# Masks of the second scores as rank-32 step products, and a plan with ranks for single operations

## The chip, the cores and the metric

The kernel runs on one core of one Trainium2 chip. The time is device microseconds from the start of the program to its end, smaller is better. Three timed runs of the kernel before are shown, and one more execution that was profiled.

## The reference

One transformer layer on x of shape (1, 4096, 256), float32: local attention with a post-norm, then a gated feed-forward part with a post-norm.

```python
# attention: 16 query heads in 4 groups, head size 16; each group has one key and one value head
q, k, v = x @ Wq + bq, x @ Wk + bk, x @ Wv + bv          # k, v: 4 heads of 16
scores = q @ k.T / sqrt(16)
mask   = (i - 128 >= j) | (i < j)                        # each query sees itself and the 127 before it
att    = softmax(where(mask, -1e9, scores)) @ v
x      = layernorm(x + att @ Wo + bo)
# feed-forward: each row is mixed with the row before it
xr, xk = mu_r * x + (1 - mu_r) * x_prev, mu_k * x + (1 - mu_k) * x_prev
out    = sigmoid(xr @ W_r.T) * (square(relu(xk @ W_k.T)) @ W_v.T)
x      = layernorm(x + out)
```

## The kernel before

The 4096 rows are cut into 32 blocks of 128 and these into 16 pairs; four blocks (512 rows) are a chunk. Per chunk the kernel transposes x (`xT`, L560), makes keys and values (`kv`, L583) and queries (`q`, L631), transposes the values (`vT`, L606), and moves every second query head 16 partitions up with four DMAs (`q move`, L653).

Scores are computed twice. The **first time** ("maxima", L686 to L708) they lie with queries on partitions, so that VectorE can take each row's maximum over the keys (`reduce`, L718). The negated maxima are transposed and stored by four DMAs into a row of qT (`nm put`, L732), where they act as one more element of the contraction, next to a row of ones in kT. The **second time** ("weights", L775 and L787) keys lie on partitions. The product with 17 rows then gives score minus maximum, transposed, and ScalarE only has to apply exp (L827, L855). For a block of 128 queries there are three kinds of second scores: its own keys and the previous block's keys as far as they are full width (`weights a`, one block of 128 queries, 512 columns), and the rest for two blocks together (`weights b`, L837 on, two halves of 256 columns). The exps go into the product with the values (`values`, L882 and L895), whose extra column of ones gives the denominators.

The mask of the second scores is added on TensorE. Before the product, small bf16 matmuls write 0 or -2^30 into the same PSUM columns: `identZ` (a 32 x 32 identity with 32 columns of zeros on one side) as weights spreads a mask tile (`maskOwn`, `maskPrev`, `maskNone`) into the even or odd 32 keys of the 64. There are two such passes, E and O, for each half of 64 keys and each of four head groups. A pass that masks the whole of one query tile besides the step of another has 256 columns, one that has the step alone 128.

All of this works on TensorE in tiles: row tiles of 32 by column tiles of 64 in the second scores (eight matmuls side by side), 32 by 128 in the maxima, 128 by 32 in the values, and full width in the rest.

The order of work is written by a planner (`Plan`, L141 on) when the program is built. Each operation is entered with `op`, with an engine, a length and a rank from the table `KINDS`, and with what it reads, writes and needs of buffers (`Ring`) and PSUM banks (`Banks`, eight). `run` plays a schedule through: on each engine, of the operations that could start within `WAIT` or `PE_WAIT` of the earliest, it takes the one of lowest rank; a change of tiling on TensorE costs `TURN`, 0.2. The instructions of every engine stand in this order and execute in it; the planner's times are nowhere in the program. SyncE (SP) issues nearly all DMAs in this order too. `rest` is one operation there: the three weights of the feed-forward part, Wo in four pieces, and bo.

In L775 and L787 the lines that matter are these:

```python
masks = ((intoE, maskOwn[:, 1:2], lo, 1), (intoO, maskOwn[:, 0:2], lo, 2))      # own keys
masks = ((intoE, maskPrev[:, 0:2], lo, 2), (intoO, maskPrev[:, 0:1], lo + RQ, 1))  # previous keys
```

The third entry is the first column, the fourth the number of 128-column tiles that a mask matmul writes.

Of the kernel before, what the change touches and what calls it, by code (L numbers as in the profile page):

```python
# [11 lines left out]
ALU = mybir.AluOpType  # L12
# [22 lines left out]
    "w": (PE, 0.43, -14.24),  # L35
    "w copy": (ACT, 0.62, 3.74),
    "x load": (SP, 0.5, -8.79),
    "x first": (SP, 3.3, -12.27),
    "x second": (SP, 2.5, -8.28),
    "xT": (PE, 0.43, 0.69),  # L40
    "xT copy": (ACT, 0.6, 5.02),
    "kv": (PE, 1.72, -6.04),
    "kv copy": (ACT, 0.69, -12.31),
    "vT": (PE, 0.43, -3.72),
    "vT copy": (DVE, 0.4, 1.8),
    "ones": (SP, 0.1, -12.06),
    "q": (PE, 1.72, -2.77),
    "q copy": (ACT, 0.69, -9.26),
    "q move": (SP, 2.0, -9.27),
    "maxima": (PE, 0.93, -1.84),  # L50
    "maxima 2": (PE, 0.66, -2.01),
    "reduce": (DVE, 1.14, 1.56),
    "reduce 2": (DVE, 0.81, -16.65),
    "nm turn": (DVE, 0.21, -6.03),
    "nm put": (SP, 2.0, 5.46),
    "weights a": (PE, 1.1, -0.52),
    "exp a": (ACT, 1.02, -9.82),
    "weights b": (PE, 1.3, -0.14),
    "exp b": (ACT, 1.02, 8.26),
    "values": (PE, 2.7, 0.67),  # L60
    "oN": (DVE, 1.25, -2.26),
    "rs": (DVE, 0.35, 9.56),
    "at": (DVE, 0.9, -0.26),
    "attT": (DVE, 0.44, 3.73),
    "xres": (SP, 0.5, -7.25),
    "bo": (POOL, 1.3, 19.18),
    "wo": (PE, 1.72, 2.61),
    "y": (DVE, 0.69, 9.88),
    "x1T first": (POOL, 0.25, 21.46),
    "x1T": (PE, 0.43, 3.16),  # L70
    "x1T copy": (ACT, 0.6, 10.29),
    "xd": (POOL, 1.3, -1.75),
    "xm": (DVE, 0.45, 27.04),
    "fk": (PE, 1.72, 6.41),
    "relu": (ACT, 0.6, 4.81),
    "square": (POOL, 1.07, 27.6),
    "fr": (PE, 1.72, 7.15),
    "gate": (ACT, 0.6, 13.52),
    "fv last": (PE, 0.86, 37.29),
    "y2 last": (DVE, 0.42, 26.45),  # L80
    "stats last": (DVE, 1.0, 21.07),
    "scale last": (POOL, 1.05, -29.88),
    "apply last": (DVE, 0.46, -15.48),
    "fv": (PE, 1.72, 3.74),
    "y2": (DVE, 0.69, -0.64),
    "y2 add": (POOL, 1.3, -4.68),
    "store": (SP, 0.5, -2.34),
    "rest": (SP, 4.5, 9.89),
    "stats y": (DVE, 0.6, 9.58),
    "scale y": (POOL, 1.5, 16.27),  # L90
    "apply y": (ACT, 0.6, 3.08),
    "stats y2": (DVE, 0.6, 10.75),
    "scale y2": (POOL, 1.5, -23.39),
    "apply y2": (ACT, 0.6, 23.42),
# [46 lines left out]
class Plan:  # L141
# [7 lines left out]
    WAIT = 0.39  # L149
    PE_WAIT = 0.20  # L150
    TURN = 0.2

    def __init__(self):
        self.ops = []
        self.writer, self.readers = {}, {}
        self.users, self.taker = {}, {}
        self.banks = Banks()

    def op(self, kind, base, fn, r=(), w=(), uses=(), new=(), banks=(), mode=None):
# [5 lines left out]
        rank += base  # L165
# [19 lines left out]
        self.ops.append((eng, length, rank, fn, deps, list(new), list(banks), mode))  # L185

    def run(self):
# [40 lines left out]
        while cand:  # L228
            best = {}
            for i in cand:  # L230
# [11 lines left out]
                turn = self.TURN if e == PE and ops[i][7] != last_mode else 0.0  # L242
# [9 lines left out]
            eng, length, _, fn, _, new, banks, mode = ops[i]  # L252
# [8 lines left out]
            land = eng == SP  # L261
            free[e] = s + length
            end[i] = s + (self.LAND + length if land else length)
            order.append((s, len(order), i))
            for k in nexts[i]:
                hop = 0.0 if ops[k][0] == eng and not land else self.DRAIN if eng == PE else self.HOP
                if ops[k][0] == PE and eng == PE:
                    hop = 0.0
                ready[k] = max(ready[k], end[i] + hop)
                left[k] -= 1  # L270
                if not left[k]:
                    cand.add(k)
# [7 lines left out]
def postln_block(  # L280
# [197 lines left out]
    identZ = const.tile([P, 3, Q], BF16, tag="identZ", name="identZ")  # L478
    nc.vector.memset(identZ, 0.0)
    nc.vector.tensor_copy(identZ[:, 1, :], identR[:, 0, :])  # L480
    intoE = identZ[:, 1:3, :].rearrange("p a b -> p (a b)")
    intoO = identZ[:, 0:2, :].rearrange("p a b -> p (a b)")


    nc.vector.tensor_tensor(diag, diag, after, ALU.add)
    four = diag.to_broadcast([P, GS, Q])
    maskOwn = const.tile([P, 2, GS, Q], BF16, tag="maskOwn", name="maskOwn")
    maskPrev = const.tile([P, 2, GS, Q], BF16, tag="maskPrev", name="maskPrev")
    nc.vector.memset(maskOwn[:, 0, :, :], NEG)
    nc.vector.memset(maskPrev[:, 1, :, :], NEG)  # L490
    nc.vector.tensor_scalar(maskOwn[:, 1, :, :], four, -NEG, NEG, ALU.mult, ALU.add)
    nc.vector.tensor_scalar(maskPrev[:, 0, :, :], four, NEG, None, ALU.mult)
    maskNone = const.tile([P, T], BF16, tag="maskNone", name="maskNone")
    nc.vector.memset(maskNone, NEG)
# [17 lines left out]
    def load_rest():  # L512
        for k, w in (("r", W_r), ("k", W_k), ("v", W_v)):
            load_w(ffn_l[k], w)
        for g in range(NG):
            nc.sync.dma_start(
                out=wo[32 * g : 32 * (g + 1), :, :],
# [810 lines left out]
```

## Time and profile before

| | |
|---|---|
| median of 3 timed runs | 356.84 us (355.78 to 358.21) |
| profiled execution, its own time | 357.12 us |
| span of the profile, first to last instruction | 355.4 us |
| TensorE busy (5091 matmuls) | 342.9 us, 96% |
| VectorE, ScalarE, GpSimd busy | 244.8, 179.0, 125.8 us |
| granted TensorE clock, mean | 0.99 |

PE is TensorE, PEld its weight loads (they overlap the matmuls), DVE VectorE, ACT ScalarE, POOL GpSimd, SPq the DMA issues of SyncE. A row of groups reads: line, engine, operation, tiles written and read, shapes, count, then busy time and mean ns of one, then idle time just before them and what ended it. A row of the timeline reads: start and length in us, engine, line, operation and count; rows of several instructions that run side by side are merged. A row of the windows reads: from and to, length, busy time (and number of instructions) of PE, PEld, DVE, ACT and POOL, granted TensorE clock, DMA share, GB/s. An fp32 matmul stands as two instructions. [...]

### The profile page before, as it was taken

The page shows a single profiled execution, that of the slowest core. Times are in us where ns is not written, and L with a number is a line of the kernel's source. Part 1 is how long each engine was busy: PE and PEld are TensorE (multiplying, and loading weights), DVE is VectorE, ACT ScalarE, POOL GpSimd, SP SyncE. Part 2 cuts the span into 40 slices and gives each one's busy share as a digit, 9 for nine tenths or more (in the row PEclk, how much of TensorE's full clock was granted, in tenths as well). Part 3 has the DMA queues.
Part 4 walks back from the last instruction along what each step waited for, and adds up shares of the span by engine and source line. Part 5 has one row for each costly group of instructions (what it writes and reads, how often), then busy time and mean ns, then how long its engine had stood idle before and what let it go on. Part 6 is the DMA issues. An engine that isn't in the chain of part 4 may idle for free.

```text
span 355.4 us, 11751 instructions
## 1 busy us (share of the span) xinstructions
PE 342.9 (96%) x5091; PEld 230.2 (65%) x5091; DVE 244.8 (69%) x464; ACT 179.0 (50%) x253; POOL 125.8 (35%) x223
## 2 busy tenths in 40 slices
PE   6999999999999999999999999999999999999982
PEld 5655565566747676767657676766757676667871
DVE  4146474888593898988927987388845888548554
ACT  3423537273537284647355554737456373863441
POOL 5110000412234363534315251253505352626883
PEclk9989999999999999999999999999999999999997
DMA  6855150140004101102223020320205020200011
GB/s 187 260 88 77 50 92 5 32 64 5 8 29 34 61 33 33 50 16 58 66 21 73 5 61 5 31 61 4 63 3 83 16 60 5 61 4 0 31 59 60
DMA packets 34518, 17.34 MB, mean 49 GB/s; under 512 B 20734, under 2 KB 34434, under 8 KB 34466
## 3 DMA queue, kind: packets, MB, share of 16 engines
q1 hardware_dynamic: 34288, 16.46, 20.5%
q8 instruction: 40, 0.66, 0.8%
q10 hardware_dynamic: 178, 0.13, 0.1%
q14 instruction: 12, 0.10, 0.1%
HBM read 9.97 MB, written 4.19 MB: 40 GB/s over the span
## 4 chain that ended last, share of the span: by engine, by line
PE 91%; DMA 3%; DVE 2%; ACT 1%; SPq 1%; POOL 1%; issue 1%; POOLq 0%; DVEq 0%; ACTq 0%
PE ps L1144 15%; PE ps L787 13%; PE ps L708 10%; PE ps L882 9%; PE ps L1021 8%; PE ps L631 8%; PE ps L1118 7%; PE ps L895 5%; PE ps L775 4%; PE ps L583 4%; PE ps L1054 3%; PE ps L695 2%; PE ps L560 2%; PE ps L606 1%; DMA qT<-qT 1%; DMA x<-in_L_attn_x 1%
## 5 line engine op out<-in xcount | busy, mean ns | idle before, releaser
L718 DVE TENSOR_REDUCE nm<-ps 128x6 f32<-128x960 f32 (+1 forms) x96 | 94.0, 1034 | 21.3 <-PE ps L708 20.9
L827 ACT ACTIVATE prA<-ps 128x1024 f32<-128x1024 f32 x64 | 61.7, 1023 | 38.1 <-PE ps L787 35.2
L787 PE MATMUL ps<-qT,kT 17*64 17x256 f32 (+1 forms) x1024 | 57.6, 495 | 0.0
L708 PE MATMUL ps<-kT,qT 16*128 16x160 f32 x1024 | 46.0, 305 | 0.4 <-DMA qT<-qT 0.4
L1176 POOL TENSOR_TENSOR y<-y,x 128x512 f32<-128x512 f32 x15 | 20.9, 1394 | 59.3 <-DVE y L1171 59.3
L708 PEld LDWEIGHTS ps<-kT,qT 16*128 16x128 f32 x1024 | 37.4, 185 | 2.7 <-issue 1.3
L966 POOL TENSOR_SCALAR ve_y<-mv_y 128x2 f32<-128x2 f32 x31 | 8.0, 257 | 87.6 <-DVE mv_y L961 87.3
L1090 DVE SCALAR_TENSOR_TENSOR xm<-xd,vecs,x1T 128x256 f32<-128x256 f32 x64 | 34.3, 582 | 1.4 <-POOL xd L1082 1.4
L855 ACT ACTIVATE prB<-ps 128x1024 f32<-128x1024 f32 x32 | 31.2, 1034 | 3.8 <-PE ps L787 3.8
L631 PE MATMUL ps<-xT,wq 128*128 128x512 f32 x64 | 32.4, 631 | 0.0
L1021 PE MATMUL ps<-wo,attT 128*128 128x256 f32 x128 | 31.6, 389 | 0.0
L882 PE MATMUL ps<-prA,vA 128*32 128x256 f32 x512 | 30.9, 382 | 0.6 <-DVE nm L718 0.6
L960 DVE BATCH_NORM_STATS2 st_y<-y 128x6 f32<-128x256 f32 x62 | 25.3, 408 | 8.7 <-POOL y L1176 8.2
L1082 POOL TENSOR_TENSOR xd<-x1T 128x512 f32<-128x512 f32 x16 | 16.6, 1041 | 40.6 <-ACT x1T L1067 40.6
L775 PEld LDWEIGHTS <-identZ 32*64 32x64 bf16 x1024 | 18.2, 104 | 19.5 <-issue 18.5
L1118 PE MATMUL ps<-xm,wkT 128*128 128x256 f32 x128 | 30.3, 380 | 0.3 <-ACT prB L855 0.3
L1144 PE MATMUL ps<-wrT,xm 128*128 128x256 f32 x128 | 30.4, 380 | 0.0
L1144 PE MATMUL ps<-wvT,kact 128*128 128x256 f32 x120 | 29.4, 387 | 0.8 <-ACT sig L1158 0.8
L1144 PEld LDWEIGHTS ps<-wvT,kact 128*128 128x128 f32 x120 | 22.0, 190 | 11.6 <-issue 7.5
L1012 POOL TENSOR_TENSOR xres<-xres,bo_b 128x512 f32<-128x512 f32 x16 | 20.4, 1278 | 25.2 <-DMA xres<-in_L_attn_x 13.7
L1021 PEld LDWEIGHTS ps<-wo,attT 128*128 128x128 f32 x128 | 23.2, 190 | 7.9 <-ACT prA L827 5.3
L1031 DVE TENSOR_TENSOR y<-ps,xres 128x512 f32<-128x512 f32 x16 | 11.1, 691 | 23.0 <-PE ps L1021 17.5
(99 smaller groups left out, 511.3 us busy)
## 6 DMA issues: line engine op xcount, KB each, us to landing
x<-in_L_attn_x SPq DMA_DIRECT2D x16, 256.0 KB
xres<-in_L_attn_x SPq DMA_DIRECT2D x16, 256.0 KB
out<-res SPq DMA_DIRECT2D x15, 256.0 KB
qT<-qT SPq DMA_DIRECT2D x32, 64.0 KB
qT<-nmT SPq DMA_DIRECT2D x64, 4.0 KB
wl_xk<-in_L_attn_Wq SPq DMA_DIRECT2D x1, 256.0 KB
wl_xr<-in_L_ffn_W_r SPq DMA_DIRECT2D x1, 256.0 KB
wl_xr<-in_L_ffn_W_k SPq DMA_DIRECT2D x1, 256.0 KB
```

Source lines behind the costliest of these rows:

```text
L631: nc.tensor.matmul(ps, wq[:, ch, rp, :, :].rearrange("p g x -> p (g x)"), xT[c][:, ch, :], start=(ch == 0), stop=(ch == C2 - 1),)
L708: nc.tensor.matmul(sc[g // 2][:, g % 2, u * W : (u + 1) * W], qT[c][g0 : g0 + DH, (2 * p + j) % NB, s, :, :].rearrange("p r i -> p (r i)") ...
L718: nc.vector.tensor_reduce(nms[p % 2].rearrange("p g j s -> p g (j s)")[:, 2 * i : 2 * i + 2, lo:hi], two_banks(keys[i])[:, :, 0 : n * W].r ...
L775: nc.tensor.matmul(dst[g][:, lo : lo + n * RQ], into[q, :], maskNone[q, 0 : n * RQ] if m is None else m[q].rearrange("p s r i -> p (s r i) ...
L787: nc.tensor.matmul(dst[g], kT[k, k0 : k0 + 64], qT[c][k, blk, r0 : r0 + nr, :, :].rearrange("p s r i -> p (s r i)"), start=False, stop=Tru ...
L827: nc.scalar.activation(prA[b][:, 2 * i : 2 * i + 2, :], two_banks(keys[i]), AF.Exp)
L855: nc.scalar.activation(prB[p][:, 2 * i : 2 * i + 2, :, :].rearrange("p g j n -> p g (j n)"), two_banks(keys[i]), AF.Exp,)
L882: nc.tensor.matmul(av[32 * g : 32 * (g + 1), hf, j, :], vA[:, values_of(b, g)], prA[b][:, g, hf * H : (hf + 1) * H], start=(j == 0), stop= ...
L1021: nc.tensor.matmul(ps[:, j, :], attT[2 * p + j][:, rp, :, :].rearrange("p s i -> p (s i)"), wo[:, rp, :], start=(rp == 0), stop=(rp == 1),)
L1090: nc.vector.scalar_tensor_tensor(dst[p][:, ch, :], st["d"][:, ch, :], muT[:, which, ch : ch + 1], x1T[p][:, ch, 0:H2], ALU.mult, ALU.add,)
L1118: nc.tensor.matmul(ps[:, o, :], ffnT["k"][:, ch, o * P : (o + 1) * P], xk[p][:, ch, :], start=(ch == 0), stop=(ch == C2 - 1),)
L1144: nc.tensor.matmul(ps[:, b, :], lhs[:, ch, b * P : (b + 1) * P], w[:, ch, :], start=(ch == 0), stop=(ch == C2 - 1),)
```

## The change

The masks of the second scores are written in another way. Where before each 32 keys of a 64-key half got their own mask tile, now the weights of the mask matmul are a step matrix over 64 keys (`step`, or its complement `back`), and the moving tile is one and the same: -2^30 times the identity, repeated (`negR`). A product of the two masks, for one query tile, all 64 keys at once. A half of 64 keys still takes two such products (for the first and for the second query tile of the pair that touches it), each of 128 columns in `weights a`. In `weights b` both blocks of the pair are masked by the same matmul, of 2 x 128 columns, and its two halves become one block of masks followed by one block of products. The first query block, which has no previous keys, gets a whole mask (`put_all`).

In the planner the lengths of the two weights kinds are 0.92 and 1.1 instead of 1.1 and 1.3, a weights block directly after another one costs `DRY` (0.3), `WAIT` and `PE_WAIT` are wider, DMA lengths differ, all ranks are new, and TensorE's operations get a rank for each single one from a table `ADJUST`. The one `rest` load is cut into five operations (W_k, W_r, W_v, Wo, bo), each of which the planner places by itself, and each reader waits for its own.

In the program that comes out, TensorE has 776 mask matmuls in its second scores (528 of 128 columns, 244 of 256, 4 of 512) instead of 1024 (504 of 128, 512 of 256, 8 of 512), the rest of its work is the same in number and shape, and its order is another: the two `weights a` and the `weights b` of a pair, which mostly stood close together (15 times a `weights a` directly ahead of another weights block), now have other work between them (4 times). There are 153 changes of tiling instead of 128. At the start SP issues both xres loads, x tiles 2 to 5, Wo, the ones, the move of q, x tiles 6 to 9, W_k, W_r, W_v, bo, and then the first `nm put`; before, the three weights, Wo and bo stood ahead of the move of q. The transposes of the three weights come after the first maxima instead of ahead of them.

```diff
 KINDS = {
-    "weights a": (PE, 1.1, -0.52),
-    "weights b": (PE, 1.3, -0.14),
-    "rest": (SP, 4.5, 9.89),
+    "weights a": (PE, 0.92, -3.74),
+    "weights b": (PE, 1.1, -0.16),
+    "rest": (SP, 1.4, 29.33),
+    "rest wo": (SP, 2.0, 28.31),
+    "rest bo": (SP, 0.8, 34.95),
...
+ADJUST = {
+    "weights b": [
+        -8.25, -1.85, -1.15, -1.05, -0.05, 0.8, 1.25, -5.4, -5.55, -4.35, 4, 0.4, 1.95, 2.15, 9.15, -12.25,
+    ],
...
-        rank += base
+        n = self.count[kind] = self.count.get(kind, -1) + 1
+        rank += base + (ADJUST[kind][n] if kind in ADJUST else 0)
...
+    def turn(self, before, after):
+        return self.TURN if before != after else self.DRY if after == "32x64" else 0.0
...
-    identZ = const.tile([P, 3, Q], BF16, tag="identZ", name="identZ")
...
-    maskNone = const.tile([P, T], BF16, tag="maskNone", name="maskNone")
-    nc.vector.memset(maskNone, NEG)
+    step = const.tile([P, 4, Q], BF16, tag="step", name="step")
+    back = const.tile([P, 4, Q], BF16, tag="back", name="back")
+    nc.vector.memset(step[:, 0, :], 0.0)
+    nc.vector.tensor_copy(step[:, 1, :], after[:, 0, :])
+    nc.vector.memset(step[:, 2:4, :], 1.0)
+    nc.vector.tensor_scalar(back, step, -1.0, 1.0, ALU.mult, ALU.add)
+    negR = const.tile([P, NS, GS, Q], BF16, tag="negR", name="negR")
+    nc.vector.tensor_scalar(
+        negR.rearrange("p s r i -> p (s r) i"), diag.to_broadcast([P, NS * GS, Q]), NEG, None, ALU.mult
+    )
+    FIRST, SECOND, ALL = slice(Q, 3 * Q), slice(0, 2 * Q), slice(2 * Q, 4 * Q)
...
+    def put_masks(dst, own, first, second, start=(True, True)):
+        for i, (part, cols) in enumerate(((FIRST, first), (SECOND, second))):
+            for h in range(len(dst)):
+                for g in range(len(dst[h])):
+                    q = slice(32 * g, 32 * (g + 1))
+                    d = dst[h][g][:, :, cols[h] : cols[h] + RQ]
+                    nc.tensor.matmul(
+                        d,
+                        flat(step if own[h] else back)[q, part],
+                        negR[q, 0 : d.shape[1], :, :].rearrange("p s r i -> p s (r i)"),
+                        start=(i == 0 and start[h]),
+                        stop=False,
+                        skip_group_check=True,
+                    )
...
-            half_scores(b, [two_banks(k) for k in keys], slice(0, T), ((1, 0, NS), (0, 0, NS)), True)
+            sc = [two_banks(k) for k in keys]
+            dst = [[sc[g // 2][64 * h : 64 * (h + 1), g % 2, :] for g in range(NG)] for h in range(2)]
+            if b:
+                put_masks(
+                    [[d.rearrange("p (o n) -> p o n", o=1) for d in half] for half in dst],
+                    (True, False), (0, 2 * RQ), (RQ, 3 * RQ),
+                )
...
+            for h in range(2):
+                put_scores(dst[h], b, h, 1 - h, 0, NS)
...
+            if p:
+                put_masks(dst, (False, True), (0, 0), (RQ, RQ))
...
             for j in range(2):
-                half_scores(
-                    2 * p + j,
...
+                for h in range(2):
+                    put_scores([d[:, j, :] for d in dst[h]], 2 * p + j, h, h, 2 * h, 2)
...
-        op("w", base, turn, r=["rest"], w=[("wps", k)], banks=[(key, 1)], mode="full")
+        op("w", base, turn, r=[("rest", k)], w=[("wps", k)], banks=[(key, 1)], mode="full")
...
-            op("rest", 0, load_rest, w=["rest"])
+            for k in ("k", "r", "v", "bo", "wo"):
+                op("rest" if k in ffn_l else "rest " + k, 0, lambda k=k: load_rest(k), w=[("rest", k)])
```

`put_scores` is the old product loop (L787) as a function of its own, `put_all` one mask matmul per head group over all columns.

## The prediction

> **What bounds the kernel now.** I read the page first (engines, slices, chain), then the groups of instructions by shape, then the timeline of one steady stretch on TensorE, then the windows and queues of the start.
>
> ```profile
> span 355.4 us, 11751 instructions
> PE   6999999999999999999999999999999999999982
> PE 91%; DMA 3%; DVE 2%; ACT 1%; SPq 1%; POOL 1%; issue 1%; POOLq 0%; DVEq 0%; ACTq 0%
> ```
>
> The chain that ended last is 91% TensorE, and from the second slice to the last but one TensorE never rests. The windows say it more sharply: from 100 to 300 us it is busy 199.98 of 200. So every nanosecond of its stream is path, and work on the other engines counts only where TensorE must wait for it. The groups of the second scores (masks L775, products L787):
>
> ```profile
> L787 PE MATMUL ps<-qT,kT 17*64 17x512 f32 x512 | 34.9, 599 | 0.0
> L787 PE MATMUL ps<-qT,kT 17*64 17x256 f32 x512 | 22.9, 391 | 0.0
> L775 PE MATMUL ps<-maskPrev,identZ 32*64 32x256 bf16 x248 | 19.2, 280 | 0.0
> L775 PE MATMUL ps<-maskOwn,identZ 32*64 32x256 bf16 x256 | 18.6, 267 | 0.0
> L775 PE MATMUL ps<-maskOwn,identZ 32*64 32x128 bf16 x256 | 16.4, 227 | 0.0
> L775 PE MATMUL ps<-maskPrev,identZ 32*64 32x128 bf16 x248 | 15.0, 213 | 0.0
> ```
>
> 70 us of mask matmuls is not 70 us of path: eight run side by side (four row groups, two column groups). What they cost is seen only in the order of starts:
>
> ```profile
> 120.84 0.25 PE L775 MATMUL ps<-maskOwn,identZ 32*64 32x128 bf16 x4
> 120.85 0.30 PE L775 MATMUL ps<-maskPrev,identZ 32*64 32x256 bf16 x4
> 120.92 0.28 PE L775 MATMUL ps<-maskOwn,identZ 32*64 32x256 bf16 x4
> 120.99 0.22 PE L775 MATMUL ps<-maskPrev,identZ 32*64 32x128 bf16 x4
> 121.08 1.12 PE L787 MATMUL ps<-qT,kT 17*64 17x512 f32 x16
> 122.13 1.99 PE L1144 MATMUL ps<-wvT,kact 128*128 128x256 f32 x8
> ```
>
> A first-scores block starts at 120.84, its products at 121.08, the next block at 122.13: masks 0.24, block 1.29. Within it, a pass of 128 columns is followed after 0.08 (120.84 to 120.92) and one of 256 after 0.14 (120.85 to 120.99), so 128 columns more cost 0.055.
>
> **The scores themselves.** From start to start of all such blocks in the timeline: 17 first-scores blocks that go over to other work take 22.3 us (mostly 1.29; 1.18 at 197.97, where the products start after 0.19), 15 followed directly by another scores block 16.0 (1.05), and 16 second-scores blocks 24.2 (0.60 for the first half, 0.94 for the second). Together 62.4.
>
> *First scores after.* Masks: 16 matmuls as before, all of 128 columns; each column group streams 256 columns instead of 384. That is one step of 0.055 less; the product, 0.86 (512 columns), stays. I take 0.054: 1.29 becomes 1.24 for the first block of a pair of query blocks, 1.18 becomes 1.13 for a later one, 1.05 becomes 1.00. The gain can't be more than the whole second pass (about 0.1), and is nothing if issue, not streaming, sets the products' start.
>
> *Second scores after.* One block instead of two halves: 16 masks of 256 columns instead of 32 of mixed width, then both products. Masks 0.13 + 0.11 = 0.24, products 2 x 0.43 (as in 0.60 less 0.19), 0.13 for going over (1.18 against 1.05): 1.23. Why now 1.54 and not 1.32 (0.60 twice and 0.13)? In the second half the starts lie 0.016 apart, not 0.003: after 64 instructions the queue runs dry. The new block has 96 instructions instead of 128. Bounds: 1.19 with no loss, 1.40 if most of the dry loss stays.
>
> *In the new order* 28 of the 32 first-scores blocks go over to other work and 4 stay. Sum: 16 x 1.24 + 12 x 1.13 + 4 x 1.00 = 37.4, second scores 16 x 1.23 = 19.7, and 0.5 for the scores blocks that still stand behind another one (now 1.42 and 1.50 on leaving, against 1.29): 57.6. **Saved: 4.8.**
>
> **What the new order costs.** The changed program has 153 changes of tiling on TensorE, now 128. The row first: a full-width block takes 1.73 before another full one and 1.82 before a tiled one, a first-scores block 1.05 staying and 1.18 to 1.29 leaving, a two-unit maxima block 0.67 before another maxima and 0.87 to 1.15 otherwise. The Trainium skill speaks against this change: *TensorEngine Tiling (Array Packing)*, section Tiling Modes, says that changing the tiling mode drains the engine, so separating scores blocks buys drains. It gives no price. Taken with the dearest row, 0.24 for each of 25 more, it would be 6.0 and the change would lose. By the rows it is less: the leaving of scores blocks is counted above, 10 more full-to-tile entries at 0.09 are 0.9, three more lone two-unit maxima at 0.2 are 0.6. **Lost: 1.5.** The rest of the PE blocks are the same in number and shape.
>
> **Waits.** Starts exceed these plain durations by 9.3 us in the trace: 2.2 for the first x tiles, 0.9 for the move of q, 1.6 for slow clock, 1.9 for the two last gates, 2.7 in small pieces. I laid the same durations (exp 0.97, reduction 1.09, 0.2 from a matmul to its reader, 0.1 otherwise) along both orders, every block behind its producers, its buffers and its banks: 9.6 us of idle with the old order (slow clock not in it), 10.0 with the new, in 28 places of 0.1 to 0.6 besides the start. I take no difference. The waits have not gone, they stand elsewhere; that is an estimate.
>
> **The start.**
>
> ```profile
> 8.65 0.46 SPq L370 DMA_DIRECT2D wl_xr<-in_L_ffn_W_r  x1
> 15.87 3.32 SPq L653 DMA_DIRECT2D qT<-qT  x4
> 21.86 0.67 PE L708 MATMUL ps<-kT,qT 16*128 16x160 f32 x9 [0.40 <-DMA qT<-qT]
> 24.20:27.62 3.42, 3.42 (x5) 0.99 (x5) 2.34 (x3) 0.00 (x0) 0.00 (x0) 0.53 0.02 4
> ```
>
> The three FFN weights (256 KB each) and bo now stand ahead of the move of q; in the new order only Wo does, and the weights come after it and after x tiles 6 to 9: 1.8 MB. The move, landing 2.7 after its last issue, then meets an emptier queue: I take 0.3 of its 0.9 wait back (bounds 0 and 0.9). The weights start at about 20 and at 297 GB/s (window 8 to 16) need 6 us; x and W_k are there by 25, W_v by 27. The new order transposes W_k after two maxima, q, kv, maxima, at about 26.8, W_v at 29.4: hidden with 2 us to spare; without that cover TensorE, in order, would stand for the lateness. Behind them on SP is the first store of row maxima, needed from about 29.5: clear. Per-weight loads let each transpose wait for its own matrix, worth nothing where all have landed. The setup on VectorE loses eight instructions (about 1.6 us) and gains five (about 0.9 by like rows), all inside its 4.31 us of idle before L611: nothing. POOL and ACT do what they did.
>
> The last row is the second place for the skill: TensorE ran at 0.53 of its clock from 24.20 to 27.62, two q matmul pairs taking 3.45 instead of 1.72. *TensorE: Matmul & The Clock Gate*, in its table on why this matters, warns of idle gaps over about 3 us; by that rule there should be no drop here, since TensorE was busy 3.8 of the 4.2 us before it. The row says that a loose stretch can be enough. By the rule the new start would gain 1.6, by the row it keeps it; the new start also waits for q, so I keep it and put 1.6 into the range.
>
> **Sum.** 4.8 - 1.5 + 0.3 = 3.6. The profiled execution took 357.12 (span 355.4 and 1.7 around it), so 353.5 there; from the median 356.84, **353.2**. About 1% (3.6 us) is what a measurement of this kernel can tell from no change, so this sits on the edge.
>
> **Rivals.**
> *Likeliest: the stream shortens* by 2 to 5.5 us (351.3 to 354.9). For it: TensorE has no slack to absorb anything, and the widths are fixed by the program. Chance 0.63; about three quarters of it lies beyond 1%, or with the clock drop gone.
>
> *Issue, not streaming, sets the masks.* Mask count in first scores is unchanged (16), so their blocks stay at 1.29 and 1.18 (16 x 1.29 + 12 x 1.18 + 4 x 1.05 = 39.0), and second scores only fall to 1.40 (22.4): with the 0.5, 61.9, so 0.5 saved, 1.5 lost, 0.3 won: 357.5. For it: the 0.016 spacing in the dry half. Against: 0.003 between starts wherever the queue was full. That is also the case in which the change doesn't do what it says. Chance 0.23.
>
> *Slower: banks.* A scores block takes four of the eight PSUM banks until two exps of 0.97 have read it. The old order repeats one pattern, and L1021 waits behind exps for some 0.4 (PEld idle 5.3 in 13). The new order has no pattern; if scores blocks come where the exps before are not done, each pair of blocks loses one more exp, 0.6 net: 16 x 0.6 = 9.6, so 356.84 - 3.6 + 9.6 = 362.8. It decides from 0.23 per pair on. Against it: ACT is busy 50% only, and the laid-out waits don't grow. Chance 0.14.
>
> **Numbers.** Faster by over 1%: 0.47 of the likeliest. Within 1%: 0.15 of it and the second rival, with 0.02 of the third: 0.40. Slower by over 1%: 0.13. The range leaves out some 0.05 below 351 and 0.14 above 358.6.
>
> **What would show it.** Right: products start 0.13 to 0.19 after the first mask of a first-scores block, second scores last 1.2 to 1.3, TensorE's busy time falls by 3 to 4 us, full blocks before tiled ones stay at 1.82. Wrong: products still at 0.19 to 0.24; second scores at 1.4; idle of TensorE before weights, values or wo, ended by ACT, of more than 3 us in sum; a wait at the weight transposes for their DMA; leaving a tiling at more than 0.25.

## The result, and the profile after

The changed kernel took 359.9 us (median; 357.19 to 362.15) where the kernel before, on the same chip, took 357.48. The ratio is 1.0076 (95%: 1.0053 to 1.0100): slower by some 2.7 us, where 3.6 us of gain were forecast. (Ratios here and below come from all runs of both kernels and so differ a little from the quotient of the medians.) Repeated on another chip it gave 1.0066 (1.0042 to 1.0090). The profiled execution took 358.53, its span is 356.8. The span is 1.4 longer than before, so this execution shows only part of the loss; the rest differs from run to run, and we come back to it.

The page of the changed kernel, with its span and the chain that ended last:

```profile
span 356.8 us, 11231 instructions
PE 85%; DVE 4%; ACT 3%; DMA 3%; POOL 2%; issue 1%; SPq 0%; POOLq 0%; DVEq 0%; ACTq 0%
```

TensorE's share of the chain fell from 91% to 85%: part of what it no longer streams, it waits. The window from 100 to 300 us says the same, first before and then after:

```profile
100.00:300.00 200.00, 199.98 (x3186) 134.53 (x3179) 153.78 (x276) 107.42 (x151) 77.69 (x136) 1.00 0.17 37
100.00:300.00 200.00, 197.59 (x3009) 128.19 (x3012) 150.47 (x274) 104.28 (x145) 81.33 (x134) 1.00 0.14 35
```

The scores blocks did become shorter. Blocks are counted from start to start; a row's recorded length can reach past the next start. A second-scores block of the kernel before, its two halves and the next block:

```profile
125.10 0.28 PE L775 MATMUL ps<-maskPrev,identZ 32*64 32x256 bf16 x4
...
125.70 0.38 PE L775 MATMUL ps<-maskPrev,identZ 32*64 32x256 bf16 x5
...
126.65 1.99 PE L1021 MATMUL ps<-wo,attT 128*128 128x256 f32 x8
```

TensorE's timeline of the changed kernel, a second-scores block (from its first mask at 124.31 to the next work at 125.53), a later first-scores block (154.36 to 155.47), and the first one of a pair of query blocks (116.77 to 118.06):

```profile
124.31 0.30 PE L832 MATMUL ps<-negR,back 32*64 32x256 bf16 x4
124.55 1.05 PE L860 MATMUL ps<-qT,kT 17*64 17x256 f32 x32
125.53 0.66 PE L1133 MATMUL ps<-ident,x 128*128 128x128 f32 x4
...
154.36 0.25 PE L832 MATMUL ps<-negR,step 32*64 32x128 bf16 x4
154.49 1.04 PE L860 MATMUL ps<-qT,kT 17*64 17x512 f32 x16
155.47 0.48 PE L1223 MATMUL ps<-wvT,kact 128*128 128x256 f32 x1
...
116.77 0.25 PE L832 MATMUL ps<-negR,step 32*64 32x128 bf16 x4
117.01 1.12 PE L860 MATMUL ps<-qT,kT 17*64 17x512 f32 x16
118.06 0.48 PE L1197 MATMUL ps<-xm,wkT 128*128 128x256 f32 x1
```

The second scores take 1.22 here (1.55 before, 125.10 to 126.65; 1.54 in most), the later first scores 1.11 (1.18), but the first block of a pair is at 1.29 as it was: its products start 0.24 after its first mask although the masks are narrower.

And this is the start on TensorE, two lines of the kernel before and then the changed kernel:

```profile
20.67 0.23 PE L695 MATMUL ps<-maskM,identR 32*128 32x128 bf16 x4
22.25 0.38 PE L686 MATMUL ps<-mask,identR 32*128 32x480 bf16 x3
```

```profile
19.91 0.23 PE L759 MATMUL ps<-maskM,identR 32*128 32x128 bf16 x4
21.71 1.14 PE L772 MATMUL ps<-kT,qT 16*128 16x160 f32 x11 [0.54 <-DMA qT<-qT]
22.57 0.24 PE L750 MATMUL ps<-mask,identR 32*128 32x160 bf16 x3
24.10 3.45 PE L695 MATMUL ps<-xT,wq 128*128 128x512 f32 x4
27.39 1.88 PE L647 MATMUL ps<-xT,wkv 128*128 128x512 f32 x4
```

The two-unit maxima block that needs the move of q (the four DMAs that move every second query head) lasts from 19.91 to 22.57, 2.66, where one that waits for nothing takes 0.67. It stands 2.0 for the move, which was 0.9 before (1.57, 20.67 to 22.25). The q pair after it takes 3.29 instead of 1.82: half clock, as in the trace before the change.

### The profile page after: what moved, and what is told of

Read it like the earlier page. It is cut to its first block, busy times and chain, and to the rows that moved or that the text cites. A ratio compares the mean times of both kernels' runs of the same rounds, so it can differ in the third digit from the quotient of the medians.

```text
span 356.8 us, 11231 instructions
## 1 busy us (share of the span) xinstructions
PE 342.2 (96%) x4843; PEld 221.9 (62%) x4843; DVE 243.8 (68%) x461; ACT 179.2 (50%) x253; POOL 129.3 (36%) x223
## 4 chain that ended last, share of the span: by engine, by line
PE 85%; DVE 4%; ACT 3%; DMA 3%; POOL 2%; issue 1%; SPq 0%; POOLq 0%; DVEq 0%; ACTq 0%
PE ps L1223 14%; PE ps L860 11%; PE ps L772 9%; PE ps L961 8%; PE ps L695 8%; PE ps L1100 7%; PE ps L1197 7%; PE ps L974 5%; PE ps L647 4%; PE ps L832 3%; DMA qT<-qT 3%; PE ps L1133 2%; PE ps L624 2%; PE ps L759 2%; DVE nm L782 2%; ACT prA L897 1%
## 5 line engine op out<-in xcount | busy, mean ns | idle before, releaser
L860 PE MATMUL ps<-qT,kT 17*64 17x256 f32 (+1 forms) x1024 | 52.1, 488 | 0.0
L772 PE MATMUL ps<-kT,qT 16*128 16x160 f32 x1024 | 48.0, 304 | 0.9 <-DMA qT<-qT 0.9
L772 PEld LDWEIGHTS ps<-kT,qT 16*128 16x128 f32 x1024 | 38.9, 185 | 2.8 <-DMA qT<-qT 1.8
L1045 POOL TENSOR_SCALAR ve_y<-mv_y 128x2 f32<-128x2 f32 x31 | 8.8, 285 | 84.6 <-DVE mv_y L1040 83.7
L1169 DVE SCALAR_TENSOR_TENSOR xm<-xd,vecs,x1T 128x256 f32<-128x256 f32 x64 | 31.8, 545 | 4.3 <-POOL xd L1161 3.8
L1255 POOL TENSOR_TENSOR y<-y,x 128x512 f32<-128x512 f32 x15 | 19.4, 1292 | 26.9 <-DVE y L1250 26.9
L986 DVE STREAM_TRANSPOSE oN<-ps 128x1024 f32<-128x1024 f32 x16 | 20.0, 1250 | 12.0 <-PE ps L974 12.0
L1197 PEld LDWEIGHTS ps<-xm,wkT 128*128 128x128 f32 x128 | 23.7, 190 | 7.2 <-issue 1.6
L1223 PEld LDWEIGHTS ps<-wrT,xm 128*128 128x128 f32 x128 | 23.5, 190 | 5.2 <-issue 1.0
```

What stands on the lines that cost most here:

```text
L772: nc.tensor.matmul(sc[g // 2][:, g % 2, u * W : (u + 1) * W], qT[c][g0 : g0 + DH, (2 * p + j) % NB, s, :, :].rearrange("p r i -> p (r i)") ...
L860: nc.tensor.matmul(dst[g], kT[k, k0 : k0 + 64], qT[c][k, blk, r0 : r0 + nr, :, :].rearrange("p s r i -> p (s r i)"), start=False, stop=Tru ...
L1169: nc.vector.scalar_tensor_tensor(dst[p][:, ch, :], st["d"][:, ch, :], muT[:, which, ch : ch + 1], x1T[p][:, ch, 0:H2], ALU.mult, ALU.add,)
L1197: nc.tensor.matmul(ps[:, o, :], ffnT["k"][:, ch, o * P : (o + 1) * P], xk[p][:, ch, :], start=(ch == 0), stop=(ch == C2 - 1),)
L1223: nc.tensor.matmul(ps[:, b, :], lhs[:, ch, b * P : (b + 1) * P], w[:, ch, :], start=(ch == 0), stop=(ch == C2 - 1),)
```

## The experiments

Ratios are to the kernel before on the same chip, with their 95% intervals. "The masks" are the step products without the new order, "the order" is the new planner with everything that it reads.

**Masks alone, order alone.** The first applies only the hunks on masks to the kernel before; the second is the changed kernel with the old mask products; the third issues the three FFN weights and bo ahead of Wo and the move of q again, as before the change; the fourth is the changed kernel once more.

```diff
# e1_masks: kernel before
-    half_scores(...)            # L775: identZ, maskOwn, maskPrev, maskNone
+    put_masks(...), put_scores(...)   # step, back, negR; ranks, lengths, loads as before
# e2_order: changed kernel
-    put_masks(...), put_scores(...)
+    half_scores(...)
# e3_early: changed kernel, order of issue on SP
+        early = [i for i in seq if self.kinds[i] in ("rest", "rest bo")]
+        seq = [i for i in seq if i not in early]
+        at = [self.kinds[i] for i in seq].index("rest wo")
+        for i in seq[:at] + early + seq[at:]:
```

> The old order of work and the old places, with the new mask products alone. Theory (the stream of TensorE shrank as forecast and the new order gave it back in waits): first scores followed by others fall from 1.05 to 1.00, second scores directly behind them from 1.54 to about 1.28, that is 0.31 per pair of query blocks and 5.0 us in all, so about 352.5 against 357.5, and the waits stay as they were. Rival (the shorter masks are taken up by the next wait, so the masks are worth nothing on the path): 357 to 358, with the waits of TensorE grown by what the stream lost.

> The new order of work, with the old mask products. Theory: dearer than the changed kernel by the masks, 1.18 instead of 1.11 for a first-scores block and about 1.48 instead of 1.25 for second scores, 5 us in all: about 365, and so 7 us over the kernel before for the order alone. Rival (masks worth nothing): about 360, as the changed kernel.

> The changed kernel, with the loads of W_k, W_r, W_v and bo issued ahead of Wo and so ahead of the move of q; the order on all other queues is unchanged. If what is queued behind the move of q slows it (x tiles 6 to 9 and then the weights), the wait of the first maxima falls from 2.0 to 1 to 1.5 us: 358.9 to 359.4. If what is queued ahead slows it, the wait grows to 2.5 or more: 360.5. If neither, 359.9.

> The changed kernel again, on the same chip as the three others, to compare with: 359.9 if nothing of the chip enters. If the drops of the clock make its spread, its single runs lie one window (3.4 us at half clock, 1.7 us) apart and go with the mean clock.

| kernel | median us | ratio |
|---|---|---|
| e1_masks | 356.46 | 0.9978 (0.9960 to 0.9995) |
| e2_order | 359.74 | 1.0070 (1.0040 to 1.0100) |
| e3_early | 359.97 | 1.0092 (1.0055 to 1.0128) |
| r_after | 359.36 | 1.0066 (1.0042 to 1.0090) |

The order costs 2.5 us (1.4 to 3.6), where 7 were expected, and the masks seem worth almost nothing: 0.8 in the old order, 0.4 in the new. Where the weights stand in the queue is not what hurts. But the traces of e1_masks and of the kernel before have the same blocks in the same order, so they can be laid over each other block by block. From 28 us to the end e1_masks gains 2.5 us steadily; before 28 us it had lost 3.1. Two things to explain, then: why 2.5, and what happens at the start.

*Why 2.5.* TensorE's timeline of e1_masks, a second-scores block directly behind a first-scores block, and one behind a full-width block:

```profile
127.05 0.28 PE L768 MATMUL ps<-negR,back 32*64 32x256 bf16 x4
127.27 1.17 PE L796 MATMUL ps<-qT,kT 17*64 17x256 f32 x32
128.46 1.99 PE L1036 MATMUL ps<-wo,attT 128*128 128x256 f32 x8
...
78.23 0.30 PE L768 MATMUL ps<-negR,back 32*64 32x256 bf16 x4
78.47 1.05 PE L796 MATMUL ps<-qT,kT 17*64 17x256 f32 x32
79.45 0.26 PE L695 MATMUL ps<-maskM,identR 32*128 32x128 bf16 x4
```

1.41 (127.05 to 128.46) against 1.22 (78.23 to 79.45; also 1.22 at 111.50, ahead of a full-width block). Behind a scores block the products of one round start up to 0.14 apart; behind another block they start within 0.02. Twelve of the sixteen blocks stand like that in the old order, and win 0.13 each, not 0.31. The changed kernel parts them, which is what its `DRY` price is for, and pays for it in changes of tiling. With the first blocks of pairs, which win nothing, that is why the masks gain so little. That an instruction queue runs dry there, as `DRY` and the prediction's "dry loss" have it, is a reading; no run tests it.

**The price of a change of tiling.** To the kernel before, one small matmul is added in the middle of each of 63 full-width blocks, 32 x 64 in the first kernel, full width in the second. Its result is overwritten by the next matmul.

```diff
# p_tile, in wo, fk, fr, fv, ahead of the second half's first matmul
+                nc.tensor.matmul(ps[0:64, 1, 0:64], maskNone[0:32, 0:64], maskNone[0:32, 0:64], ...)
# p_full
+                nc.tensor.matmul(ps[:, 1, 0:64], maskNone[:, 0:128], maskNone[:, 0:64], ...)
```

> The kernel before, with one small matmul put between the two halves of each of 63 full-width blocks (wo, fk, fr, fv): 32 rows, 64 columns of weights, 64 columns streamed, into the half that the next matmul starts anew. It adds 126 changes of tiling and nothing that anybody waits for. The price of a change is the difference to the same kernel with a full-width small matmul in the same places. Theory (a change costs 0.11 wherever it stands, as the two orders' durations give: 2.7 us for 25 more): 126 x 0.11 = 13.9 us between the two, 12 to 16. Rival 1 (what scores blocks pay on leaving belongs to them, not to the change): 0 to 4 us. Rival 2 (a full drain, 0.24 each): 30 us.

> The same 63 small matmuls, full width (128 rows, 128 columns of weights, 64 columns streamed): no change of tiling. 63 times about 0.06 to 0.1: 4 to 6 us above the kernel before, by either theory. Theory: 12 to 16 below the one with changes of tiling; rival 1: 0 to 4 below; rival 2: 30 below.

Measured: 378.37 (ratio 1.0620, 1.0584 to 1.0655) and 363.20 (1.0199, 1.0157 to 1.0241). The difference is 15.2 us for 126 changes: 0.12 each (the two intervals leave about 2 us either way, so 0.10 to 0.14). The two timelines, p_tile and then p_full:

```profile
126.11 1.13 PE L1150 MATMUL ps<-wvT,kact 128*128 128x256 f32 x4
127.17 0.21 PE L1148 MATMUL ps<-maskNone 32*64 32x64 bf16 x1
127.31 1.13 PE L1150 MATMUL ps<-wvT,kact 128*128 128x256 f32 x4
```

```profile
126.37 1.13 PE L1023 MATMUL ps<-wo,attT 128*128 128x256 f32 x4
127.34 0.19 PE L1021 MATMUL ps<-maskNone 128*128 128x64 bf16 x1
127.36 1.11 PE L1023 MATMUL ps<-wo,attT 128*128 128x256 f32 x4
```

The half block ahead takes 1.06 into a tile and 0.97 into full width (0.09 for going in); the small matmul itself takes 0.14 against 0.02 (0.12 for coming out). By this price the new order's 25 more changes cost 25 x 0.12 = 3.0, an estimate: the price was measured in the old order, between the halves of full-width blocks. The order's 2.5 is of that size, but other terms are in it too (see the part on why).

**The start: loads.** Four loads that nobody needs for long are moved behind the weights on SP (s_), and three more x tiles from right behind the move of q to after the second ones (t_): with old masks and old order, with new masks and old order, and (s_ alone) in the changed kernel.

```diff
# s_before, s_e1, s_after: order of issue on SP
+        xr = [i for i in seq if self.kinds[i] == "xres"][:2]
+        xl = [i for i in seq if self.kinds[i] == "x load"][2:4]
+        ... # xl + xr behind "rest" (s_after: behind "rest wo")
# t_before, t_e1: besides
+        hold = [i for i in seq if self.kinds[i] == "x load"][4:7]
+        ... # hold behind the second "ones"
```

> The kernel before, with only four loads moved in the queue of SP: the first two residual tiles and x tiles 4 and 5, which nobody needs before 28 us, are issued behind W_r, W_k, W_v, Wo and bo instead of between x tiles 1, 2 and 3. Theory 'start' (x tile 2, which TensorE waited for, comes earlier; in the trace of the kernel before that wait was 0.7 us, in that of the old order with new masks 2.4): about 0.5 to 1 below the kernel before, ratio 0.997 to 0.999, and a narrower spread. Rival (the start is bounded by the whole amount of data, or something else is late next): no change, 1.000.

> Old order with the new masks and the same four loads moved. Laid block for block beside the kernel before, the old order with new masks won 2.5 us between 30 and 350 us, and lost 3.1 before 28 us (x tile 2 landed late, two stretches at half clock). Theory 'start': with x tile 2 early this loss goes, and the 2.5 show: 2.2 to 3 us below the same kernel with old masks and the same loads, ratio to the kernel before about 0.990 to 0.993. Rival (the masks' gain is taken back wherever the kernel starts): ratio 0.997 to 0.999, under 1 us below.

> The changed kernel with the same four loads moved behind Wo (the FFN weights stay where the change put them, behind the move of q). Theory 'order': the new order costs 2.7 in TensorE's stream and about 0.7 at the end, the masks give 3.0; if part of the loss was the start, the ratio to the kernel before falls to 1.000 to 1.003. Rival (the start has no part in it): 1.006 to 1.008 as the changed kernel has now.

> Old masks, old order, the four loads moved as before, and x tiles 6, 7 and 8 issued behind the second load of ones (about 24 us) instead of right behind the first move of q. Theory (the move of q shares the queues with these tiles, lands late, and the wait for it and the thin stretch around it bring the half clock): the wait of 0.4 at 21 us goes, nearly no run has the half clock before 30 us; 0.5 to 1 below the four moved loads alone, about 354, the mean granted clock at 0.996 or more in nine runs of ten. Rival (the move's own 64 KB in small packets set its landing): no change to the four loads alone, 355.0.

> The same with the new masks in the old order. Theory (the masks' gain was hidden by the start alone): 2.2 to 3 below the same start with old masks, about 351.5, ratio to the kernel before 0.984 to 0.987. Rival (the half clock comes with the new masks however the loads lie, as in 19 of 22 runs with the four loads moved): 355, under 1 us from the same start with old masks.

| kernel | median us | ratio | mean granted clock over its runs |
|---|---|---|---|
| s_before | 354.99 | 0.9968 (0.9947 to 0.9989) | 0.9946 |
| s_e1 | 355.77 | 0.9963 (0.9942 to 0.9984) | 0.9914 |
| s_after | 360.16 | 1.0095 (1.0058 to 1.0132) | 0.9870 |
| t_before | 355.22 | 0.9969 (0.9954 to 0.9984) | 0.9960 |
| t_e1 | 354.25 | 0.9921 (0.9890 to 0.9951) | 0.9946 |

The four loads are worth 1 us and do nothing for the changed kernel; holding back three more (t_before) adds nothing to that. The theory that they hid the masks' gain fell with s_e1: it was to be 2.2 to 3 below s_before and was 0.8 above it in the medians. With the three more held back the masks won 1.7 (0.9921 against 0.9969), still short of that. Two clues remained. The clock: runs of the kernel before average 0.9932, runs of the changed one 0.9880, and each stretch of 3.4 us at half clock costs 1.7 us. Of 28 runs of the changed kernel 13 are at 0.986 or less (around 360.3 us), of 111 of the kernel before 12 are. The clock doesn't tell all: r_after's profiled execution took 360.16 at a mean of 0.996. Stretches of the changed kernel's trace and then two of r_after's:

```profile
23.80:27.20 3.40, 3.40 (x6) 1.50 (x5) 2.74 (x3) 0.00 (x0) 0.00 (x0) 0.52 1.01 319
```

```profile
10.20:13.60 3.40, 3.40 (x5) 1.33 (x4) 0.00 (x0) 0.44 (x1) 0.00 (x0) 1.00 0.63 171
23.80:27.20 3.40, 2.87 (x47) 2.16 (x47) 1.47 (x2) 0.00 (x0) 0.00 (x0) 1.00 1.05 284
```

In r_after the first kv pair took 3.57 (9.34 to 12.91; 1.83 in the other trace) under a recorded clock of 1.00, so some half-speed work is not in the record, and the q pair behind its wait of 2.0 ran at full speed. The second clue is the wait for the move of q: in four pairs of traces that differ in the masks alone the maxima block was 0.55 to 0.69 longer with the new masks, in both orders, although in t_before and t_e1 the first of the move's DMAs is issued at the same 15.48 us.

**The start: where the tiles lie.** The new mask tiles take 1536 bytes a partition, the old ones 2240. All tiles allocated after them lie 704 bytes lower in SBUF, qT at byte 98848 of each partition instead of 99552 (places by the program's layout; no trace holds an address). Three kernels put back or leave the place:

```diff
# t_pad: t_e1 and; a_pad: the changed kernel and (r_te1: t_e1 again)
+    pad = const.tile([P, 352], BF16, tag="pad", name="pad")     # 704 bytes, never read
+    nc.gpsimd.memset(pad[:, 0:2], 0.0)
```

> New masks, old order, all loads moved as in the best start so far, and one unused tile of 704 bytes a partition behind the new mask tiles. The new masks take 1536 bytes a partition where the old took 2240, so every tile allocated after them, qT among them, lies 704 bytes lower; with the unused tile all of them lie where they lay before. In four pairs of traces that differ in the masks alone, the two-unit maxima block that waits for the first move of q was 0.55 to 0.69 longer with the new masks (2.20 against 1.57, 2.34 against 1.65, 2.06 against 1.41, 2.66 against 2.10). Theory 'place' (the move, SBUF to SBUF, lands later because qT lies elsewhere): the block falls back to about 1.4, the half clock at 24 to 28 us becomes rare, and the median falls from about 354.2 to 353, ratio to the kernel before about 0.990. Rival (it comes with the masks or the shorter set-up on VectorE, not with the place): block 2.06, median and ratio as without the unused tile, 0.992.

> The same without the unused tile, once more, for comparison on the same chip: 354.2, ratio to the kernel before 0.990 to 0.994, the maxima block at 2.06 in its trace, by either theory.

> The changed kernel with the same unused tile, so that its tiles lie where they lay before the change, as in the kernel with the new order and the old masks. Theory 'place': the maxima block of 2.66 falls to 2.1, fewer runs have two stretches at half clock; median 0.5 to 1.5 below the changed kernel, ratio to the kernel before 1.002 to 1.005. Rival (place has no part): ratio 1.006 to 1.008.

| kernel | median us | ratio |
|---|---|---|
| t_pad | 352.49 | 0.9887 (0.9846 to 0.9928) |
| r_te1 | 354.58 | 0.9932 (0.9907 to 0.9956) |
| a_pad | 356.84 | 1.0003 (0.9973 to 1.0032) |

The changed kernel with 704 unused bytes is level with the kernel before. TensorE's timeline at its start, beside which the lines of the changed kernel above should be held:

```profile
19.97 0.23 PE L761 MATMUL ps<-maskM,identR 32*128 32x128 bf16 x4
21.57 0.67 PE L774 MATMUL ps<-kT,qT 16*128 16x160 f32 x9 [0.31 <-DMA qT<-qT]
21.95 0.24 PE L752 MATMUL ps<-mask,identR 32*128 32x160 bf16 x3
23.30 1.98 PE L697 MATMUL ps<-xT,wq 128*128 128x512 f32 x4
25.12 1.88 PE L649 MATMUL ps<-xT,wkv 128*128 128x512 f32 x4
```

The maxima block takes 1.98 instead of 2.66, and the q pair after it 1.82 instead of 3.29: the half clock is gone in this execution, the fastest of the kernel's 14. A later move is affected too: the maxima block that ends at 275.71 in the changed kernel took 1.51, waiting for its move; the same block here takes 0.92.

**Does the place act by itself, and what about it counts?** The kernel before with its tiles shifted, and three more places for the new masks.

```diff
# b_shift: the kernel before, 320 bytes     # t_p192, t_p256, t_p480: t_e1
+    pad = const.tile([P, 160], BF16, tag="pad", name="pad")      # [P, 96], [P, 128], [P, 240]
+    nc.gpsimd.memset(pad[:, 0:2], 0.0)
```

> The kernel before, nothing changed but an unused tile of 320 bytes a partition behind its mask tiles, so that qT begins at 99872 instead of 99552: 32 bytes past a multiple of 512, as in the changed kernel (98848), where it was 224 past one. Theory 'place': the old masks in the old order lose as the new ones did: the maxima block that waits for the move of q takes 2.2 instead of 1.57, and the time is 1.5 to 2.5 above the kernel before, ratio 1.004 to 1.007. Rival (only the new masks suffer): ratio 1.000.

> New masks, old order, all loads moved, with an unused tile of 192 bytes: qT begins at 99040, 224 past a multiple of 512 and 96 past one of 128, as in the kernel before, though all tiles lie 512 lower than there. Theory 'place within 512 bytes': as with 704 bytes, 352.5, block 1.46. Rival (the absolute place or a neighbour counts): 354.4, block 2.06, as without.

> The same with 256 bytes: qT begins at 99104, 32 past a multiple of 128 and 256 as without an unused tile, but 288 past a multiple of 512. If the place within 128 or 256 bytes counts: 354.4, block 2.06, as without. If the place within 512 counts: between, or 352.5.

> The same with 480 bytes: qT begins at 99328, a multiple of 512, where all the 128-byte pieces of its move are aligned. If a piece that crosses a 64-byte line costs, this is the best place: under 352.5, block under 1.46. If only 224 past a multiple of 512 is good: 354.4.

| kernel | qT begins at | past a multiple of 256 | first maxima block that waits, us | median us | ratio |
|---|---|---|---|---|---|
| before | 99552 | 224 | 1.57 | 356.84 | 1 |
| b_shift | 99872 | 32 | 2.18 | 359.35 | 1.0044 (1.0025 to 1.0063) |
| t_e1 | 98848 | 32 | 2.06 | 354.25 | 0.9921 (0.9890 to 0.9951) |
| t_p256 | 99104 | 32 | 2.06 | 353.85 | 0.9907 (0.9876 to 0.9939) |
| t_p192 | 99040 | 224 | 1.40 | 352.54 | 0.9869 (0.9834 to 0.9904) |
| t_pad | 99552 | 224 | 1.46 | 352.49 | 0.9887 (0.9846 to 0.9928) |
| t_p480 | 99328 | 0 | 0.66 | 351.87 | 0.9843 (0.9811 to 0.9875) |

The kernel before, with not one instruction of its work changed, loses 1.6 us (0.44%) when its tiles shift by 320 bytes; its block went to 2.18 as expected. And the place within 256 bytes orders the block, and within the t_ kernels the medians: 32 is worst, 224 better, 0 best (0 and 224 overlap in their intervals). With qT aligned the wait is gone altogether. The starts of t_e1 and of t_p480 on TensorE:

```profile
20.29 0.23 PE L705 MATMUL ps<-maskM,identR 32*128 32x128 bf16 x4
22.34 0.38 PE L696 MATMUL ps<-mask,identR 32*128 32x480 bf16 x3
24.21 3.56 PE L641 MATMUL ps<-xT,wq 128*128 128x512 f32 x4
```

```profile
20.31 0.23 PE L707 MATMUL ps<-maskM,identR 32*128 32x128 bf16 x4
20.97 0.53 PE L698 MATMUL ps<-mask,identR 32*128 32x480 bf16 x4
22.75 1.88 PE L643 MATMUL ps<-xT,wq 128*128 128x512 f32 x4
```

In each the three lines are the block that needs the move, the next maxima block, and the q pair (its length 3.56 against 1.88). In the second nothing waits and the q pair runs at full clock. t_p480, new masks in the old order with the loads moved and the tiles aligned, beats both kernels: 351.87 against 357.52 for the kernel before on its chip, 1.6% (1.25 to 1.9) faster.

An unused tile shifts all tiles behind it, but the traces' semaphore events show the move itself, which reads and writes qT alone: from the start of the issue of its fourth DMA to that DMA's last event, the first move takes 4.3 to 4.6 us in all ten traces with qT at 32, 3.4 to 3.75 in all nine at 224, and 2.44 at 0, with old and new masks and in both orders. The packets tell where: one of 128 bytes takes 24 ns at 224 and 11 at 32 and 0, but at 32 (t_e1) the last event comes 2.2 us behind the last packet, at 0 (t_p480) 0.4. So it is the place of qT that slows the move.

The Trainium skill has a rule for this: *DMA: Bandwidth & Descriptors*, section "How a descriptor splits into AXI transactions", says that a transaction must start at a multiple of 256 bytes, so that a descriptor which crosses one becomes two. The move reads 128 bytes at every 256 from qT's first byte on and writes 128 bytes behind each. With qT at 0, neither piece crosses a multiple of 256; at 224 the piece that is read does (224 to 352), at 32 the piece that is written (160 to 288). By the 32-byte beats of its table I estimate 224 as the dearest (11 + 7, against 5 + 9 at 32 and 4 + 8 at 0); the runs agree with it on 0 (2.44), and put a crossing write (4.3) above a crossing read (3.5). That reading fits all seven rows; other places within 256 were not tried.

## Why the prediction was wrong

Three parts add up to the loss, each measured by itself: the masks gain about 2.9 (t_pad against t_before with the tiles in the same place: ratios 0.9887 and 0.9969; 2.4 in the new order, a_pad against e2_order), the order costs 2.5 (e2_order, tiles as before), and the shifted tiles cost 2.2 to 2.6 (1.0066 and 1.0076 against 1.0003). Sum +1.8 to +2.2; measured +2.4 and +2.7; each part is known to some 1.1 to 1.6 us. The shifted tiles are the largest single cause of the loss beside the order's and were in no term of the prediction, but they are not the whole of it: without them (a_pad) the change would still have been level, not 3.6 faster. Term by term, in the profiled executions:

- **The start** is the step that failed in its mechanism. The move "then meets an emptier queue: I take 0.3 of its 0.9 wait back (bounds 0 and 0.9)": the wait rose to 2.0. The queue has no part in it: the fourth DMA of the move lands 3.67 us after its issue in the kernel before, 3.72 in e2_order, where less stands ahead of it, 4.43 in the changed kernel, and 4.44 in e3_early, with the weights ahead again. Of the rise, some 0.5 is the order's (TensorE reaches the block at 19.63 in e2_order, at 20.67 before) and 0.6 the place's. The step counted the eight removed and five added set-up instructions and the 1.8 MB of loads, but not that fewer bytes of mask tiles move every later tile. It also took the half-clock stretch as one fixed 1.6 us: it comes once, twice or not at all from run to run. It was there in both profiled executions, which differ by 1.4, where the runs differ by 2.4 to 2.7; that a longer wait makes it more frequent is likely (last part), not shown.
- **Saved: 4.8** in the scores was 3.5: blocks sum to 59.0 in the changed kernel against 62.5, where 57.6 was forecast. First scores came out as forecast in sum (38.0; the first of a pair stayed at 1.29, the later ones fell further, to 1.11). Second scores were the mis-sized term: 21.1, not 19.7, mean 1.32. The 1.23 holds (1.22 in five) behind full-width or values blocks, and two more take 1.29; the three behind a scores block take 1.35 to 1.38, and the five behind maxima 1.39 to 1.48, in which a wait of the next block is contained. (In its sum 0.43 for a product is 0.60 less 0.17, the row of a half behind another one, not less 0.19.)
- **Lost: 1.5** for the order came out. The trace of e2_order is 3.0 longer than the one before; its scores blocks take 0.5 more (63.0 against 62.5), the first maxima block that waits 0.5, the end 0.6, which leaves about 1.5 for all other blocks, waits included. Weighing the row of 0.09 against the dearest of 0.24 was sound: the price is 0.12 (p_tile), half of the bound that the prediction worked out for the Trainium skill's rule (*TensorEngine Tiling (Array Packing)*, section Tiling Modes) that a change drains the engine.
- **"I take no difference" in waits** was too kind. Starts exceed plain durations by 2.7 us more than before, not counting the scores blocks; 1.0 of it is the start. In e2_order they are 0.7 above the kernel before, with the same order and slower masks, so the rest comes with the shorter masks and the shifted tiles: TensorE now arrives earlier than exps and reductions, and the moves land later. The largest is this, in the changed kernel, after two second-scores blocks in a row:

```profile
186.03 0.26 PE L759 MATMUL ps<-maskM,identR 32*128 32x192 bf16 x4 [0.83 <-ACT prB L934]
```

- **The end** was not in the forecast: from the last product's start to the last store's issue it takes 5.3 in the new order (348.41 to 353.69) and 4.7 in the old (347.95 to 352.67), since the normalization of the last but one pair now shares VectorE and GpSimd with the last. Scores 1.3 short, the start 1.3, the other waits 1.7 and the end 0.6 make 4.9 of the 5.0 by which the span missed its forecast (1.4 more instead of 3.6 less).
- **Rivals.** "Issue, not streaming, sets the masks" was given 357.5 and comes closest to a_pad's 356.84, by luck and with half of its reasons: the first blocks of pairs did not move, and neither did the second scores behind a scores block move as far as their streaming would let them. "Banks" is real once (the line above) and not 0.6 a pair: idle of TensorE ended by ACT after 30 us is about 1.8 in all. The case that came true, tiles shifted under a DMA, was none of the three.

What stays open: a_pad's trace has a span of 353.5, 1.9 under the kernel before, and its median is level with it. Of the 1.9, 1.7 is the half-clock stretch, which the trace before has and this one lacks. The runs of a_pad average a granted clock of 0.9902, those of the kernel before on that chip 0.9936; what brings the lower clock in the new order was not tried.

## What to carry to other kernels

A change that resizes a tile in SBUF is also a change of the address of every tile after it: look at what small-piece DMAs read and write there, and compare with the old addresses restored by an unused tile before judging the change. A gain read from one shape of block holds only where the block stands between the same neighbours; sum it by neighbour. And where TensorE's order is parted to spare a stall, price both sides: here 0.14 to 0.19 for a second-scores block behind another scores block against 0.12 for each change of tiling that parting them adds.

## What the runs showed of the hardware

- A move from SBUF to SBUF in pieces of 128 bytes, read at every 256 and written 128 behind, took from the issue of its last DMA 4.3 to 4.6 us with its tile 32 bytes past a multiple of 256, 3.4 to 3.75 with it 224 past, and 2.44 on a multiple of it; the block that waits for it took 2.0 to 2.7, 1.4 to 2.1 and 0.66. Issuing the three weights ahead of it changed nothing (4.43 without, 4.44 with them).
- A change between full width and 32 x 64 tiles on TensorE cost 0.12 us each (15.2 us for 126), without any wait on another engine.
- A stretch of some 3.4 us at half TensorE clock (0.52 and 0.53 granted) stood some 2 us behind a wait of 0.9 to 2.0. Of eleven traces whose first maxima block took over 2 us, nine have it there, and the two others had worked at half speed before 16 us; of nine with a shorter block, two have it. That the wait brings it is likely, not shown. The Trainium skill (*TensorE: Matmul & The Clock Gate*, section "Why this matters for your kernels") warns of idle gaps of over about 3 us; here the drop came behind far shorter ones.
